# Absolute value of the spread positions two steps later and pinned in ScalarE's order, and nine buffers for the projection's loads

## The chip, the core and the metric

The kernel runs on one core of a Trainium2 chip, in fp32. The metric is the device time of one launch in microseconds; the median of three runs is given. TensorE is written PE below (PEld: its weight loads), VectorE DVE, ScalarE ACT, GpSimd POOL and SyncE SP.

## The reference, cut to what matters

Two layers on 32 images of 96 x 56 x 56. The first is an inverted bottleneck with residual; the second an attention by spectrum and a deformable convolution:

```python
# layer 0
h = silu(bn(conv1x1(x, fake_quant(w1))))           # 96 -> 576
h = silu(bn(depthwise3x3(h, fake_quant(w2))))
s = sigmoid(se_w2 @ silu(se_w1 @ h.mean((2, 3)) + se_b1) + se_b2)
x = x + bn(conv1x1(h * s, fake_quant(w3)))         # 576 -> 96
# layer 1
ca, sa = ...            # channel and spatial attention, from rfft2(x) and x
y = x * ca * sa
aux = concatenate([y, coord, freq_e])              # freq_e from rfft2(y)
offset = conv3x3(aux, off_w) + off_b               # 9 taps, (x, y) each
gate = sigmoid(conv1x1(relu(conv3x3(aux, dg1_w) + dg1_b), dg2_w) + dg2_b)
y_base = conv3x3(y, base_w) + base_b
px, py = xx + offset[:, :, 0], yy + offset[:, :, 1]
sampled = grid_sample_taps(y, px, py)              # bilinear: weights 1 - |distance|, cut at 0
y_def = einsum('bcthw,oct->bohw', sampled, def_w) + def_b
z = (1 - gate) * y_base + gate * y_def
out = relu(batch_norm(z over all images) + x)
```

## The kernel before

**Bands.** The second layer runs in bands of eight rows, seven to an image, 224 in all, in the loop at the end of `layers` (counted 0 to 6 in an image; a turn of the work beside it, described below, starts two bands before the end of an image, and the example that is read closely, from about 2160 us on, is one such turn). For band n, two halves are sampled: `sample_tiles` multiplies blocks of the image with a table of bilinear weights (L700, PE) and copies the results out of PSUM (L704, ACT); `pack` copies channels into the free partitions (three L711, ACT); `deform` multiplies with the deformable weights (seven L719, PE: the first needs the L704 copies alone, the others the packed ones). `combine` (L745 to L748, DVE) mixes in gate and base convolution. `block_channels` makes the blocks (POOL copy L682, transposes L686, ACT copy L688).

**The positions, two bands ahead.** `find(n + 2)`, which is the generator `offsets`, runs during band n and is advanced one step at a time: one `next` at the band's start, then seven for each half, each beside one `pump`. At the band's end a loop runs it out. Its steps: the joint convolution (L582, nine matmuls, and the base convolution L611), the offsets to `at` (L630, DVE), to DRAM as `od` (L634, POOL), and from there as `ht` to 112 partitions (L646, SP, 252 KB: each position is spread over the possible source columns and rows). Then ACT takes the absolute distance (L649, Abs) and cuts it (L650, Relu of 1 - |d|), and the result goes to DRAM as `hd` (L653, on ACT's queue). `weights_load` reads it back as `wc` and `wr`, two loads each to a half (L664 and L665, SP, 252 KB each), and `weights` multiplies them (L671, DVE) to the table that L700 uses.

**What runs beside it.** `pump` also advances two streams over other images, each by its share of the band's slots: `first(b + 2)` is `hidden` (expansion L166 on PE, L170 on ACT; depthwise taps L257 and L259 on DVE; Silu L219 on ACT, whose store L221 is on ACT's queue) and `second(b + 1)` is `attend`: the projection (`project_loads` L307 on SP into the pool `hq`, five loads of 196 KB to a set, matmuls L323, ACT L325, POOL add L443), then the spectra (loads L351 on SP, matmuls L376, squares L360 on ACT, reductions L362 on DVE, copies L383 on ACT, and so on) and the maps of attention. `load_rows` fetches the next image's rows (L561, SP), `attend_rows` (L569, DVE) multiplies them in place.

**Who sets the order.** SP runs in the order of the program (`manual_schedule`). For the other engines a scheduler chooses an order at compile time, by its own estimate of when operands are ready[...]. Buffers are rings: an `hq` load has to wait until the matmul that read the buffer eight loads back is done. The convolutions and the sampling share six PSUM banks (`bank`, pool `mm`); `acc` and `pd` have one each.

## Time and profile before

| | us |
|---|---|
| median of three runs (lowest, highest) | 9928.33 (9917.45, 9945.53) |
| profiled execution | 9938.35 |
| its span | 9936.6 |
| PE busy | 8753.8 |
| DVE busy | 7220.3 |
| ACT busy | 5346.3 |
| POOL busy | 2785.4 |

The mean granted clock of PE in the profiled execution is 0.933. The DMA engines moved 1485.53 MB, 150 GB/s. The span is nearly uniform: images pass through it at about one in 290 us, all with the same order of work. So one image is read closely, and the sums of the whole run are divided by 32. A row of the timeline gives the start, the length, the engine, the line, the operation with output and input tiles, how many instructions were put together, and in brackets the idle time of the engine before it with what ended it. A line of the waits gives the same over the whole run: the sum, the number of waits and the longest.

### The profile page before, as it was taken

How to read it: one execution, taken by the hardware profiler on the slowest of the kernel's cores; microseconds unless marked ns; L12 is line 12 of the kernel's file. 1: busy time of each engine (PE TensorE's matmuls, PEld its weight loads, DVE VectorE, ACT ScalarE, POOL GpSimd, SP SyncE). 2: the span in 40 equal slices, each digit the busy share in tenths (PEclk: the TensorE clock that was granted, in tenths of full speed). 3: DMA queues.
4: the chain of work that ended last, by engine and by line, in shares of the span. 5: the costliest groups of instructions: out<-in, count | busy, mean ns of one | idle time of the engine just before them, and what ended most of it. 6: DMA issues, size and time to landing. Idle time of an engine off the chain costs nothing. (4 is left out here: it accounts for less than half of the span.)

```text
span 9936.6 us, 122378 instructions
## 1 busy us (share of the span) xinstructions
PE 8753.8 (88%) x43766; PEld 5029.2 (51%) x43766; DVE 7220.3 (73%) x6948; ACT 5346.3 (54%) x10262; POOL 2785.4 (28%) x2639
## 2 busy tenths in 40 slices
PE   6899999998999999999899989999999999999970
PEld 3455555555555555555555555555555555555550
DVE  6688777777777777877777877777777777778323
ACT  2355555555555555555555555555555555555443
POOL 1132323332322333232233233233323223322210
PEclk9899999999999999999999999999999999999985
DMA  3345555554555555555555555555545555545549
GB/s 93 108 134 144 147 148 151 149 139 132 148 148 150 152 150 134 148 143 150 153 147 146 140 142 149 151 146 148 143 134 149 148 151 152 148 132 145 129 142 418
DMA packets 1085588, 1485.53 MB, mean 150 GB/s; under 512 B 606670, under 2 KB 856222, under 8 KB 1072686
## 3 DMA queue, kind: packets, MB, share of 16 engines
q1 hardware_dynamic: 875011, 985.23, 38.2%
q10 hardware_dynamic: 153675, 329.79, 8.9%
q0 software_dynamic: 56288, 162.60, 6.7%
q8 instruction: 352, 5.77, 0.3%
q14 instruction: 262, 2.15, 0.1%
HBM read 1064.28 MB, written 412.65 MB: 149 GB/s over the span
## 5 line engine op out<-in xcount | busy, mean ns | idle before, releaser
L259 DVE SCALAR_TENSOR_TENSOR acch<-hp,w,acch 128x1512 f32<-128x1512 f32 (+1 forms) x2250 | 4231.6, 1881 | 34.6
L682 POOL COPY ybl<-yp 96x448 f32<-96x448 f32 x896 | 1201.2, 1367 | 2065.8 <-PE mm L686 2065.3
L719 PE MATMUL pd<-v,c_def 128*96 128x224 f32 (+1 forms) x6272 | 1491.5, 391 | 315.0 <-ACT v L711 175.1
L582 PE MATMUL mm<-yp,c_jointW 104*128 104x448 f32 x4032 | 1609.2, 550 | 3.5 <-DMA yp<-fqd 3.5
L719 PEld LDWEIGHTS pd<-v,c_def 128*96 128x96 f32 (+1 forms) x6272 | 1100.7, 181 | 644.0 <-ACT v L711 192.8
L700 PE MATMUL mm<-wc,yt 64*96 64x144 f32 x12544 | 1124.4, 296 | 90.6 <-DVE yb L616 43.9
L323 PE MATMUL mm<-hq,w3s 128*96 128x392 f32 (+1 forms) x2560 | 1038.2, 546 | 168.7 <-DMA hq<-h2d 160.5
L582 PEld LDWEIGHTS mm<-yp,c_jointW 104*128 104x128 f32 x4032 | 762.3, 191 | 761.5 <-issue 694.7
L166 PE MATMUL mm<-xt,w 96*128 96x392 f32 (+3 forms) x2688 | 1077.4, 536 | 46.0 <-issue 33.0
L704 ACT COPY v<-mm 96x288 f32<-96x288 f32 (+1 forms) x2688 | 1005.8, 440 | 152.6 <-PE mm L700 120.2
L700 PEld LDWEIGHTS mm<-wc,yt 64*96 64x96 f32 x12544 | 861.9, 160 | 400.9 <-issue 233.5
L170 ACT ACTIVATE hp<-mm,sh,inv 128x392 f32<-128x392 f32 (+2 forms) x1216 | 816.0, 673 | 221.0 <-PE mm L166 143.2
L611 PE MATMUL mm<-yp,c_base0W 96*64 96x448 f32 x4032 | 916.7, 551 | 0.0
L671 DVE TENSOR_TENSOR wc<-wc,wr 128x1008 f32<-128x1008 f32 x448 | 551.9, 1232 | 458.0 <-DMA wr<-hd 349.3
L219 ACT ACTIVATE acch<-acch,sh,inv 128x1568 f32<-128x1568 f32 x288 | 486.9, 1690 | 642.2 <-DVE acch L259 641.1
L711 ACT COPY v<-v 32x448 f32<-32x448 f32 x1344 | 755.3, 562 | 28.7
L323 PEld LDWEIGHTS mm<-hq,w3s 128*96 128x96 f32 (+1 forms) x2560 | 410.1, 175 | 705.3 <-issue 576.6
L634 POOL DMA_DIRECT2D od<-at x224 | 185.9, 830 | 2046.4 <-DVE at L630 1655.6
L443 POOL TENSOR_TENSOR o<-o,xc 96x392 f32<-96x392 f32 x256 | 395.1, 1543 | 958.4 <-ACT o L325 955.9
L397 PE MATMUL mm<-s,c_GV 112*112 112x464 f32 x1536 | 659.5, 571 | 4.5 <-ACT s L383 4.5
L688 ACT COPY yt<-mm 128x384 f32<-128x384 f32 (+1 forms) x896 | 347.3, 439 | 500.1 <-PE mm L686 484.2
L569 DVE SCALAR_TENSOR_TENSOR yp<-yp,ca,sab 96x448 f32<-96x448 f32 x255 | 157.2, 626 | 576.7 <-DMA yp<-x1d 409.8
(191 smaller groups left out, 9184.6 us busy)
## 6 DMA issues: line engine op xcount, KB each, us to landing
h2d<-acch ACTq DMA_DIRECT2D x288, 784.0 KB
wc<-hd SPq DMA_DIRECT2D x896, 252.0 KB
wr<-hd SPq DMA_DIRECT2D x896, 252.0 KB
hq<-h2d SPq DMA_DIRECT2D x1024, 196.0 KB
x<-x1d SPq DMA_DIRECT2D x768, 98.0 KB
ht<-od SPq DMA_DIRECT2D x224, 252.0 KB
hd<-ht ACTq DMA_DIRECT2D x224, 252.0 KB
xt<-in_x SPq DMA_DIRECT2D x64, 609.0 KB
```

What stands on the lines that cost most here:

```text
L166: nc.tensor.matmul(pt[p0 : p0 + w1.shape[1], : rows * W], w1, xts[hf][:, r0 * W : (r0 + rows) * W], start=True, stop=True)
L170: nc.scalar.activation(h1[lo:hi, row0 : row0 + rows, 1 : 1 + W], pt[lo:hi, : rows * W].rearrange("p (h w) -> p h w", h=rows), AF.Silu, bia ...
L259: nc.vector.scalar_tensor_tensor(acc[:, lo:hi], win, wk, acc[:, lo:hi], ALU.mult, ALU.add)
L323: nc.tensor.matmul(pt[:C, :EW], w3s[ps, ch], hq[ps], start=(i == 0), stop=(i == NCH - 1))
L397: nc.tensor.matmul(pt[: 2 * W, :n].rearrange("p (q u) -> p q u", q=NPB), w["GV"][:, g], m, start=(k == 0), stop=(k == 1))
L582: nc.tensor.matmul(view, weights[:, k], yp[:channels, r0 : r0 + RB, dx + PD - 1 : dx + PD - 1 + W], start=(k == 0), stop=(k == NTAP - 1))
L611: nc.tensor.matmul(pb[k % 2 * BC : (k % 2 + 1) * BC, :BW].rearrange("p (h w) -> p h w", h=RB), w["base"][:, k], yp[:C, r0 : r0 + RB, dx + ...
L682: nc.gpsimd.tensor_copy(yb[:, :, s], blocks)
L700: nc.tensor.matmul(pt[k][:C, (t - lo) * KP : (t - lo + 1) * KP], yt[ps, t], s[ps, t * KP : (t + 1) * KP], start=True, stop=True)
L704: nc.scalar.copy(v[:C, :, lo:hi, k].rearrange("c k t p -> c t k p"), pt[k][:C, : (hi - lo) * KP].rearrange("c (t k p) -> c t k p", t=hi - ...
L711: nc.scalar.copy(v[C:, 1 + 2 * i : 3 + 2 * i], v[i * QC : (i + 1) * QC, KA:])
L719: nc.tensor.matmul(out.rearrange("c q (t x) -> c t q x", x=TS), p["w"]["def"][ks, k], v[ks, k].rearrange("c t s (r x) -> c t (s r) x", r=T ...
```

## The change

The Abs is called after six `yield`s in place of four, so it is two steps later among the 15 `next`s of a band: it was called in step 13 and is now called after the last, and the Relu with it. The store of `hd` falls from step 14 to the loop that runs the generator out at the band's end. The load of `ht` stays in step 9. `keep_in_program_order` binds the Abs behind the ScalarE instruction that was traced just before it, in order alone; `p` gets the entry `tc` for that. The pool `hq` has nine buffers in place of eight.

```diff
@@ def offsets @@
     nc.sync.dma_start(ht.rearrange("q n k -> q (n k)"), src)
-    for _ in range(4):
+    for _ in range(6):
         yield
-    nc.scalar.activation(ht, ht, AF.Abs, bias=w["blk"])
+    p["tc"].keep_in_program_order(nc.scalar.activation(ht, ht, AF.Abs, bias=w["blk"]))
     nc.scalar.activation(ht, ht, AF.Relu, bias=w["one"], scale=-1.0)
     yield
@@ def layers @@
-        p = {"dp": ctx.enter_context(tc.tile_pool(name="l1d", bufs=3, space=DRAM))}
+        p = {"tc": tc, "dp": ctx.enter_context(tc.tile_pool(name="l1d", bufs=3, space=DRAM))}
...
-        pools(tc, ctx, p, None, (("xt", 2), ("acch", 2), ("pl", 2), ("w3s", 1), ("hq", 8), ("o", 2), ("x2", 3),
+        pools(tc, ctx, p, None, (("xt", 2), ("acch", 2), ("pl", 2), ("w3s", 1), ("hq", 9), ("o", 2), ("x2", 3),
```

## The prediction

> **What bounds the kernel now.** I read the busy times first, then the waits, then one image's timeline on TensorE beside ScalarE and SyncE, then the windows view for the granted clock.

> ```profile
> PE 8753.8 (88%) x43766; PEld 5029.2 (51%) x43766; DVE 7220.3 (73%) x6948; ACT 5346.3 (54%) x10262; POOL 2785.4 (28%) x2639
> ```

> TensorE (PE) is busy 88% of the span, VectorE 73%, ScalarE 54%. A change of ScalarE's order can only pay through TensorE's idle time, and through the clock that an idle TensorE loses. Who lets it idle:

> ```profile
> ACT ht L649 <- DMA ht<-od: 736.3, 186, 9.8
> ...
> PEld pd L719 <- ACT v L711: 192.8, 74, 8.4
> ...
> PE mm L323 <- DMA hq<-h2d: 160.5, 66, 7.7
> ...
> PE pd L719 <- ACT v L704: 138.2, 35, 6.2
> ```

> The columns are total us, number of waits, longest. ScalarE stands 736.3 us at the Abs (L649), waiting for the spread positions to land. That is 23 us in each of 32 images, but ScalarE is not the bound; what counts is the smaller sum in TensorE's own rows: the deform matmuls (L719) that wait for ScalarE's copies (L711, L704), and the project matmuls (L323) that wait for their loads. In the image whose bands run from about 2160 to 2453 us, TensorE's gaps over 1.5 us are four, here called A to D:

> ```profile
> 2202.08 4.02 PE L323 MATMUL mm<-hq,w3s 128*96 128x392 f32 x10 [1.15 <-DMA hq<-h2d]
> ...
> 2241.32 5.25 PE L323 MATMUL mm<-hq,w3s 128*96 128x392 f32 x10 [4.78 <-DMA hq<-h2d]
> ...
> 2289.96 2.55 PE L719 MATMUL pd<-v,c_def 128*96 128x224 f32 x6 [8.18 <-ACT v L711]
> ...
> 2399.87 1.89 PE L376 MATMUL mm<-c_FU,x 112*112 112x116 f32 x8 [4.43 <-POOL x L356]
> ...
> 2450.13 3.30 PE L719 MATMUL pd<-v,c_def 96*96 96x224 f32 x8 [4.35 <-ACT v L704]
> ```

> The bracket is the idle time before the row and what ended it. A is the second row (with 1.15 us more before the first), B the third, C the fourth, D the fifth. ScalarE in the same stretch:

> ```profile
> 2240.78 0.78 ACT L649 ACTIVATE ht<-ht,c_blk 112x576 f32<-112x576 f32 x1 [6.15 <-DMA ht<-od]
> ...
> 2285.42 0.77 ACT L649 ACTIVATE ht<-ht,c_blk 112x576 f32<-112x576 f32 x1 [6.34 <-DMA ht<-od]
> ...
> 2289.34 1.74 ACT L711 COPY v<-v 32x448 f32<-32x448 f32 x3
> ...
> 2447.47 0.78 ACT L649 ACTIVATE ht<-ht,c_blk 112x576 f32<-112x576 f32 x1 [2.76 <-DMA ht<-od]
> ```

> At B and D the Abs itself holds the copies: at B the L711 copies that the deform matmuls need stand behind a 6.34 us wait, at D four L704 copies stand behind 2.76 us.

> ```profile
> 2281.00:2300.00 19.00, 10.82 (x33) 6.42 (x32) 16.79 (x15) 8.36 (x15) 0.00 (x0) 0.64 0.47 126
> 2445.00:2457.00 12.00, 7.65 (x40) 5.38 (x37) 10.17 (x8) 4.29 (x9) 2.43 (x2) 0.72 0.64 152
> ```

> In the last three columns (granted clock, DMA share, GB/s) the clock is 0.64 around B and 0.72 around D. Ten project matmuls take 5.25 us after A and 4.02 us after the short gap: a gap costs its length and slow work behind it.

> [...] copies whose data are ready stand behind the Abs. [...] Here the spread load (252 KB) is issued behind four weight loads of 252 KB and takes a median of 9.5 to 11.8 us to its last packet in five of the seven bands, 3.4 and 3.5 us in bands 3 and 4, where fewer loads stand ahead of it. [...]

> **The change part by part.** It adds no instruction: in the compiled order each engine has as many as before, and SP's order is the same.

> *Abs two steps later.* Compared band by band with the old order, the static order of ScalarE repeats in 28 of 32 images. By band of this image, named by the band whose positions are found (its Abs runs two bands earlier, so band 0's is the first of the example, at 2201 us):
> - Bands 0 and 5: the Abs keeps its place, so the 7.6 us wait in band 0 stays.
> - Band 1: two instructions (L325, L170) go ahead of it. Worth nothing on TensorE, as A waits for loads.
> - Band 2 (gap B): one L711 copy, an L170, an L360 and an L383 go ahead; two L711 copies still follow. The landing (2285.4) still ends the wait, but behind it stand fewer instructions. From 2285.42 to 2289.96 is 4.5 us now; without one L711 (0.56), one L360, and one L383 it is about 2 us less.
> - Bands 3 and 4: the Abs falls 25 and 16 us later, past its landing. There was 0 and 0.9 us of wait to win. The store of the result is later too (2322 to about 2340 in band 3), and SP's weight loads behind it with it; their multiply runs at 2362.8, so they have some 10 us of slack. Cost taken 0; without that slack each microsecond would show at L671, and behind it at the sampling matmuls L700.
> - Band 6 (gap D): four L704 copies (1.29 us) go ahead of the Abs. They could start at 2444.7, when L688 ends, instead of 2448.15. L719 then waits for the next thing, the L711 copies (1.74 us) and the yp rows whose load and multiply (L569) end near 2450.5 for the following conv.

> *Side effect.* The scheduler places other instructions anew. In band 2 the Silu L219 moves from 2274.34 to between L688 (2266.76) and four L704 copies (2267.66), though its last depthwise tap on VectorE is ready only about 2271.7. So a new in-order wait of about 4 us stands on ScalarE with four PSUM copies behind it, and TensorE runs out of PSUM banks: I estimate a new gap of 3.8 us at about 2268. Also in band 2 the first L360 goes ahead of the Abs, so that the next DFT loads are issued about 6 us earlier (2280 in place of 2286.66). VectorE's multiply L671 comes one tap earlier in bands 0 and 1; in band 5 L569 goes ahead of L616, which makes L616 1.4 us later, and L700 waits for it.

> *Ninth buffer.* Each project load waits for the matmul nine back in place of eight, one matmul (some 0.4 to 0.66 us) earlier. SP sits in such loads for 25.45 us from 2160.41; everything behind it (weights, spread positions) is issued 0.66 us earlier, and one load of 196 KB comes into a stretch in which the DMA is idle.

> Sum for one image:
> - A: 0.66 us earlier issue at the 4.78 gap, as much again from the 1.15 gap: -1.3 (0 to -2.0).
> - B: -2.0 behind the landing, -0.7 for the earlier issue, and +1.1 for what of the new L219 gap isn't absorbed. Most of it is: TensorE's work before B ends at 2281.8 and could end at 2285 without a loss, as the landing is what ends B. -1.6 (+2.5 to -6).
> - C: L376 about 1.2 us earlier by the earlier loads, L616 later: -0.3 (+1.5 to -3).
> - D: gap from 4.35 to about 3.0, and half of the 2 us that the slow clock costs behind it (14 L719 matmuls take 2.81 us at full clock, 4.49 to 5.54 after such gaps), at an even chance: -2.3 (-1.0 to -4.1).

> That is -5.5 us for an image. About 30 of the 32 have this pattern: -165 us. The profiled execution took 9938.35 us (span 9936.6), so 9773; it lay 10.0 us above the median of the runs (9928.33), so I predict 9765 for the median.

> **The rivals.**
> - *Shrunk gaps keep the clock* (0.14). If B and D fall below what costs the clock, each saves 2 to 3 us more: -9.5 an image, -285 us, 9645. For: half-clock time is 1338 us in 158 windows, so it is a large sum. Against: the gaps stay at 3 us and more.
> - *The stall only changes place* (0.14). The spread load lands behind four weight loads, whatever ScalarE does, and the first project matmul waits for the first load of a set, which the ninth buffer doesn't touch. Then only D's 0.5 to 1 us is left: 9905 to 9935. For: band 0 and 5 unchanged, SP's order the same.
> - *Slower: the Silu parked ahead of the PSUM copies in band 2* (0.17). Place: ScalarE between L688 and the four L704, at about 2267. Price: 3.8 us of TensorE idle and 2.5 us for the clock it costs, 6.3 us an image. It decides when more than about 4 us of it reach B's end, because A, C and D together bring 3.9. All of it: +2.4 an image, +72 us, 10000; most of it: 9975. For: [...] the banks are six. Against: the 8.18 us of idle right behind it.

> **How the numbers follow.** The forecast has 0.55 and its own range is 9690 to 9855 (-2.5 to -8 an image). The range over the cases goes from 9645 to 9960: it leaves out the worst of the slower case and little of the best. A change under 0.3% (30 us) can't be told from none. Faster: 0.55 + 0.14 + a part of the second rival (0.03) = 0.72; same: 0.11; slower: 0.17.

> **What would show it.** In the waits, L649 on its load should fall from 736 us to about 500, L719 on L711 and L704 by a third or more, L323 on its loads by 20 to 40 us, and L704 behind a waiting L219 should appear. In the timeline, D should shrink to about 3 us, B to 6 or 7, and a new gap of about 4 us should stand some 20 us ahead of B. I am wrong if B ends later after its start, if the clock around 2270 in this image falls, or if L323 still waits as long.

## The result, and the profile after

The changed kernel takes 9790.16 us in the median (9779.04 to 9798.13, four runs), the kernel before on the same chip 9936.93 (9917.45 to 9954.24; four runs, of which the table above has the first three): a ratio of 0.9852, 95% interval 0.9829 to 0.9875. The profiled execution of the changed kernel has a span of 9792.0 us at a mean granted clock of 0.937.

Its busy times, in the first part of the page:

```profile
PE 8810.8 (90%) x43766; PEld 5029.2 (51%) x43766; DVE 7212.9 (74%) x6948; ACT 5381.4 (55%) x10262; POOL 2646.4 (27%) x2639
```

The work is the same and TensorE is busy for a larger part of a shorter span. It is also busy 57.0 us longer than before with as many matmuls, so some of them run slower. The waits of the changed kernel (sum, number, longest):

```profile
DVE wc L671 <- DMA wr<-hd: 597.5, 176, 17.8
...
ACT ht L649 <- DMA ht<-od: 347.1, 107, 9.0
...
PEld pd L719 <- ACT v L711: 187.2, 105, 4.8
...
PE pd L719 <- ACT v L711: 152.9, 71, 4.6
...
PE mm L323 <- DMA hq<-h2d: 101.9, 56, 6.3
```

Half of ScalarE's wait at the Abs is gone (736.3 us before), and the project matmuls wait a third less (160.5). L719 on L704 fell from 138.2 to 14.7. But L719 on L711 fell little, and VectorE's multiply L671 waits 597.5 us for its loads. In the kernel before it waited 349.3:

```profile
DVE wc L671 <- DMA wr<-hd: 349.3, 151, 21.8
```

TensorE's timeline in one image of the changed kernel shows the four gaps in their new size, and three that were not there:

```profile
2505.02 5.25 PE L323 MATMUL mm<-hq,w3s 128*96 128x392 f32 x10 [3.50 <-DMA hq<-h2d]
...
2535.97 2.05 PE L700 MATMUL mm<-wc,yt 64*96 64x144 f32 x12 [1.36 <-ACT v L704]
...
2551.89 1.75 PE L719 MATMUL pd<-v,c_def 128*96 128x224 f32 x8 [1.11 <-ACT v L711]
...
2594.19 1.68 PE L166 MATMUL mm<-xt,w 96*128 96x392 f32 x2 [2.03 <-ACT yt L688]
...
2660.01 1.05 PE L376 MATMUL mm<-c_FU,x 112*112 112x116 f32 x8 [0.32 <-POOL x L356]
...
2666.82 1.16 PE L700 MATMUL mm<-wc,yt 64*96 64x144 f32 x8 [1.87 <-ACT hp L170]
...
2711.37 4.79 PE L719 MATMUL pd<-v,c_def 128*96 128x224 f32 x12 [2.70 <-ACT v L711]
```

A is the first row (4.78 before), B the third (8.18), C the fifth (4.43), D the last (4.35). The second, fourth and sixth rows are new. For B these two images overstate the change: over the 27 images of the table below, TensorE's wait for L711 in B's band averages 5.72 us before and 2.76 after.

For the sums I cut the whole run into bands at the gate's matmul L727 and averaged 27 images, band by band, from TensorE's records. In each field stand the band's length and, behind it, TensorE's idle time in it, in us. B falls into band 0, C into 3, D into 4, A into 6. The columns behind the first two belong to experiments below; the last one also has the swap of two VectorE instructions that is described there. Each column is one profiled execution. A second trace of the kernel before (the run hq9 below) has 292.06 us an image and bands up to 0.43 us from the first column, and the chips differ by up to 0.5%, so differences of half a microsecond in a band are not read.

| band | before | changed | nine buffers alone | pin and nine, old place | seven steps | seven, swap, ten buffers |
|---|---|---|---|---|---|---|
| 0 | 48.58, 6.32 | 45.58, 3.22 | 46.02, 3.96 | 46.61, 3.65 | 42.64, 1.64 | 45.11, 2.25 |
| 1 | 35.67, 1.65 | 38.59, 3.04 | 35.43, 1.60 | 37.84, 2.54 | 35.68, 1.90 | 34.84, 1.59 |
| 2 | 35.54, 1.28 | 36.15, 1.44 | 35.33, 1.19 | 34.93, 0.42 | 35.65, 0.87 | 35.35, 0.92 |
| 3 | 45.43, 4.22 | 43.52, 2.01 | 45.62, 4.26 | 42.58, 2.45 | 43.35, 2.38 | 42.85, 2.37 |
| 4 | 34.44, 4.56 | 32.71, 2.98 | 34.15, 4.38 | 32.22, 2.90 | 30.49, 2.19 | 30.74, 2.39 |
| 5 | 44.43, 1.75 | 42.82, 0.56 | 43.01, 0.54 | 42.44, 0.37 | 43.78, 0.50 | 43.15, 0.00 |
| 6 | 48.43, 4.73 | 47.92, 4.24 | 47.63, 4.20 | 47.63, 4.22 | 47.67, 4.02 | 43.19, 1.55 |
| image | 292.53, 24.51 | 287.30, 17.48 | 287.20, 20.14 | 284.25, 16.56 | 279.27, 13.50 | 275.22, 11.07 |

From before to changed an image loses 7.0 us of idle time but only 5.2 us of length. Bands 0, 3, 4, 5 and 6 win 8.8 us together, bands 1 and 2 give back 3.5. The time at half clock with TensorE at work stays at 22.4 and 23.5 us, but it moves: in band 1 it rises from 1.3 to 4.4 us. By an estimate from the 12 sampling matmuls shown below (2.05 us at half clock, 0.98 at full), these 3.2 us more cost about 1.6 us, so that band 1, 2.9 us longer, has 1.4 us more idle time and the rest in slower matmuls.

### The profile page after: what moved, and what is told of

Same layout as the page of the kernel before. It is cut to its first block, busy times and chain, and to the rows that moved or that the text cites. A ratio compares the mean times of both kernels' runs of the same rounds, so it can differ in the third digit from the quotient of the medians.

```text
span 9792.0 us, 122438 instructions
## 1 busy us (share of the span) xinstructions
PE 8810.8 (90%) x43766; PEld 5029.2 (51%) x43766; DVE 7212.9 (74%) x6948; ACT 5381.4 (55%) x10262; POOL 2646.4 (27%) x2639
## 5 line engine op out<-in xcount | busy, mean ns | idle before, releaser
L259 DVE SCALAR_TENSOR_TENSOR acch<-hp,w,acch 128x1512 f32<-128x1512 f32 (+1 forms) x2250 | 4264.4, 1895 | 33.4
L682 POOL COPY ybl<-yp 96x448 f32<-96x448 f32 x896 | 1107.4, 1263 | 2047.5 <-PE mm L686 2047.0
L582 PE MATMUL mm<-yp,c_jointW 104*128 104x448 f32 x4032 | 1643.7, 560 | 6.2 <-DMA yp<-fqd 3.5
L719 PE MATMUL pd<-v,c_def 128*96 128x224 f32 (+1 forms) x6272 | 1435.4, 379 | 175.6 <-ACT v L711 152.9
L719 PEld LDWEIGHTS pd<-v,c_def 128*96 128x96 f32 (+1 forms) x6272 | 1055.9, 174 | 472.6 <-ACT v L711 187.2
L700 PE MATMUL mm<-wc,yt 64*96 64x144 f32 x12544 | 1138.6, 298 | 148.7 <-ACT hp L170 54.4
L582 PEld LDWEIGHTS mm<-yp,c_jointW 104*128 104x128 f32 x4032 | 782.8, 196 | 799.0 <-issue 734.2
L166 PE MATMUL mm<-xt,w 96*128 96x392 f32 (+3 forms) x2688 | 1105.2, 549 | 73.8 <-ACT yt L688 39.8
L323 PE MATMUL mm<-hq,w3s 128*96 128x392 f32 (+1 forms) x2560 | 1029.1, 541 | 118.2 <-DMA hq<-h2d 101.9
L671 DVE TENSOR_TENSOR wc<-wc,wr 128x1008 f32<-128x1008 f32 x448 | 560.7, 1252 | 767.0 <-DMA wr<-hd 597.5
L700 PEld LDWEIGHTS mm<-wc,yt 64*96 64x96 f32 x12544 | 863.8, 160 | 487.7 <-issue 219.5
L704 ACT COPY v<-mm 96x288 f32<-96x288 f32 (+1 forms) x2688 | 999.5, 440 | 180.1 <-PE mm L700 136.4
L170 ACT ACTIVATE hp<-mm,sh,inv 128x392 f32<-128x392 f32 (+2 forms) x1216 | 815.9, 673 | 242.0 <-PE mm L166 171.3
L219 ACT ACTIVATE acch<-acch,sh,inv 128x1568 f32<-128x1568 f32 x288 | 487.6, 1693 | 660.5 <-DVE acch L259 646.6
L711 ACT COPY v<-v 32x448 f32<-32x448 f32 x1344 | 755.1, 562 | 29.7
L323 PEld LDWEIGHTS mm<-hq,w3s 128*96 128x96 f32 (+1 forms) x2560 | 403.3, 173 | 651.4 <-issue 492.9
L688 ACT COPY yt<-mm 128x384 f32<-128x384 f32 (+1 forms) x896 | 351.5, 441 | 531.0 <-PE mm L686 527.7
L166 PEld LDWEIGHTS mm<-xt,w 96*128 96x128 f32 (+1 forms) x2688 | 370.3, 184 | 485.4 <-issue 304.2
```

Of the source, the lines that this page charges most:

```text
L166: nc.tensor.matmul(pt[p0 : p0 + w1.shape[1], : rows * W], w1, xts[hf][:, r0 * W : (r0 + rows) * W], start=True, stop=True)
L170: nc.scalar.activation(h1[lo:hi, row0 : row0 + rows, 1 : 1 + W], pt[lo:hi, : rows * W].rearrange("p (h w) -> p h w", h=rows), AF.Silu, bia ...
L259: nc.vector.scalar_tensor_tensor(acc[:, lo:hi], win, wk, acc[:, lo:hi], ALU.mult, ALU.add)
L323: nc.tensor.matmul(pt[:C, :EW], w3s[ps, ch], hq[ps], start=(i == 0), stop=(i == NCH - 1))
L582: nc.tensor.matmul(view, weights[:, k], yp[:channels, r0 : r0 + RB, dx + PD - 1 : dx + PD - 1 + W], start=(k == 0), stop=(k == NTAP - 1))
L682: nc.gpsimd.tensor_copy(yb[:, :, s], blocks)
```

## The experiments

All kernels are compared by their ratio to the kernel before, run on the same chip beside them, since that kernel's own median lay between 9887 and 9937 us on the chips used.

### The parts of the change

The first run was meant to have nine buffers and nothing else.

> Nine buffers alone, Abs where it was; the order of instructions on every engine is that of before. Theory M (the moved Abs carries the gain, because PSUM copies no longer stand behind it): 20 to 50 us under before, TensorE idle for L323 on its loads down from 160 us to about 110, Abs wait L649 still above 650 us, gap C (L376 on POOL) still 100 us or more over the run. Rival H (the earlier project loads carry the gain): 100 us or more under before, Abs wait down towards 400 us.

The kernel run under this name still had eight buffers, that is, it was the kernel before. Its ratio, 1.000 (0.9989 to 1.0011), tells nothing of the buffer; it shows how well two equal kernels agree. The run with nine, later:

```diff
-        pools(tc, ctx, p, None, (("xt", 2), ("acch", 2), ("pl", 2), ("w3s", 1), ("hq", 8), ("o", 2), ("x2", 3),
+        pools(tc, ctx, p, None, (("xt", 2), ("acch", 2), ("pl", 2), ("w3s", 1), ("hq", 9), ("o", 2), ("x2", 3),
```

> Nine buffers and nothing else: the kernel before with that one number changed (the run called hq9 had kept eight). The scheduler moves a few ScalarE and VectorE instructions with it. Theory I (the ninth buffer is worth about 1% wherever the Abs stands, as it was with six and with seven steps): 60 to 120 us under before, project loads issued ahead of the band's first matmul, gap A down to about 3 us. Rival J (it is worth something only once the Abs is out of the way): within 30 us of before.

Measured: 0.9854 (0.9818 to 0.9889), 145 us, more than the 60 to 120 us of theory I; of the theories of the first run, H has the size. One more buffer brings as much as the whole change. By the table it shortens bands 0, 5 and 6 (B, and the stretch of the projection) and nothing else; C and D stay at 4.21 and 4.37 us. The Abs waits less, 586.9 us in place of 736.3, and TensorE less for L711 (175.1 us before):

```profile
ACT ht L649 <- DMA ht<-od: 586.9, 176, 7.5
...
PE pd L719 <- ACT v L711: 112.5, 37, 7.5
```

The Abs stands where it stood, except in one band, where it now stands ahead of two more instructions. So this comes from its load, which lands earlier, and not from its order.

The other half, the Abs two steps later and pinned, with eight buffers:

> Abs two steps later and pinned, eight buffers. Theory M: 90 to 130 us under before; gaps before L719 on L711/L704 halved, L323 on its loads still about 150 us. Rival H: at most 40 us under before, as the spread load still lands late and gap B stays near 8 us.

Measured: 0.9961 (0.9943 to 0.9979), 39 us. It is far from the 90 to 130 us of M. H has the size (at most 40) but not the place: B shrank (band 0 from 48.58 to 45.87 us) without the earlier loads, while band 1 grew from 35.67 to 39.37.

Then the place without the pin, and the pin without the new place, both with nine buffers:

> As the changed kernel without the pin; the scheduler then puts thousands of ScalarE instructions in other places. Theory M, if what counts is only that the Abs is called two steps later: within 0.5% of the changed kernel. Rival P (the pin carries it, since the scheduler drags the Abs forward again): half of the gain or more is lost, 9860 us or more.

> Nine buffers and the pin, with the Abs called where it was before. In the compiled order the pin alone puts the Abs behind the four L704 copies at D, behind L325 in the projection, and parks the Silu ahead of L704, all as in the changed kernel; an Abs wait stays ahead of fewer instructions. Theory P (the pin does the work, the two steps add little): within 0.4% of the changed kernel. Rival S (the two steps are needed, so that at B and in the projection fewer PSUM copies stand behind the Abs): less than half of the changed kernel's gain over nine buffers alone.

The first gives 0.9902 (0.9884 to 0.9920), between its two forecasts, and slower than nine buffers alone; the second 0.9824 (0.9787 to 0.9861), within 0.3% of the changed kernel, as theory P has it. Without the pin the waits at C and D are back:

```profile
PE pd L719 <- ACT v L704: 140.7, 34, 6.4
...
PE mm L376 <- POOL x L356: 127.9, 32, 4.4
```

With the pin, at the old place, they are gone but for 14.7 and 25.8 us (bands 3 and 4 in the table). So the pin, and not the two steps, takes away C and D. The two steps bring nothing that shows (0.9824 without them, 0.9852 with them), and rival S asked for a part of a gain over nine buffers alone that the changed kernel does not have.

C went with an order that the scheduler changed by the way. ScalarE's half L273 of the attention map's sigmoid stands ahead of the next L170 and Silu in all the pinned kernels, and VectorE's half L274 ahead of a depthwise tap (L259, 1.84 us) that it stood behind before. VectorE before, then in the changed kernel:

```profile
2374.17 1.84 DVE L259 SCALAR_TENSOR_TENSOR acch<-hp,w,acch 128x1568 f32<-128x1568 f32 x1
2375.93 0.18 DVE L274 TENSOR_SCALAR sa<-sa 112x56 f32<-112x56 f32 x1
```

```profile
2638.51 0.19 DVE L274 TENSOR_SCALAR sa<-sa 112x56 f32<-112x56 f32 x1 [0.36 <-ACT sa L273]
```

POOL, which multiplies with that map (L356), starts 1.1 us behind the end of L273 in place of 2.2, on average over the images. No run moved these two instructions alone, so this cause is read from the orders and not shown. Part of C came back in the same band: TensorE waits 1.8 us an image at the L700 of the sixth row above.

### What was given back

Band 1 is 2.9 us longer in the changed kernel. There, on VectorE and on ScalarE, in the image shown above:

```profile
2586.75 1.21 DVE L671 TENSOR_TENSOR wc<-wc,wr 128x1008 f32<-128x1008 f32 x1 [7.74 <-DMA wr<-hd]
```

```profile
2588.60 1.01 ACT L399 ACTIVATE sq<-mm 112x464 f32<-112x464 f32 x2 [6.60 <-DVE s L400]
```

The multiply waits 7.74 us for its loads with the spectral add L400 behind it, ScalarE's square L399 waits for the add, and the copies L688 stand behind the square: that ends the 2.03 us gap at L166 above. Before the change that L400 stood ahead of the multiply, which then waited 1.24 us:

```profile
2323.13 0.64 DVE L400 TENSOR_TENSOR s<-sq 112x464 f32<-112x464 f32 x1 [0.91 <-ACT sq L399]
2325.01 1.21 DVE L671 TENSOR_TENSOR wc<-wc,wr 128x1008 f32<-128x1008 f32 x1 [1.24 <-DMA wr<-hd]
```

The experiment swaps the two in each image and leaves the order of every other engine as it is (an order-only edge in every second call; `adds` lists the L400 instructions; shortened here):

```diff
-    nc.vector.tensor_tensor(wc, wc, wr, ALU.mult)
+    i = nc.vector.tensor_tensor(wc, wc, wr, ALU.mult)
...
+    p["tc"].add_manual_dep(i.ins, p["adds"][-2].ins.name, NoSync)
```

> The changed kernel with one pair of VectorE instructions swapped in each image: the multiply L671 that waits 7.7 us for its wr load goes behind the second spectral add L400, as it stood before the change; every other engine keeps the changed kernel's order. Theory L (what is given back in the stretch after B comes from this multiply holding L400, hence ScalarE's L399 and the PSUM banks): that stretch 1.5 to 3 us shorter in each image, 45 to 90 us under the changed kernel, TensorE gaps at L166 on L688 gone. Rival B (the landing of wr itself bounds the stretch, whatever waits for it): within 15 us of the changed kernel.

Measured: 0.9807 (0.9783 to 0.9830) against 0.9852, 0.45% or some 44 us. Theory L holds in size, at its low end. In place it holds in part: in the profiled execution band 1 is only 1.0 us shorter, and bands 0 and 6 are 0.6 and 0.7 us shorter too, little more than the traces differ by themselves. TensorE's wait at L166 in band 1 falls from 1.21 to 0.08 us, but its wait at L416 for VectorE's L413, which comes behind the swapped pair, rises from 1.41 to 2.32. In the same place of an image of this run:

```profile
2841.71 0.64 DVE L400 TENSOR_TENSOR s<-sq 112x464 f32<-112x464 f32 x1 [1.08 <-ACT sq L399]
...
2843.78 1.21 DVE L671 TENSOR_TENSOR wc<-wc,wr 128x1008 f32<-128x1008 f32 x1 [1.42 <-DMA wr<-hd]
```

A second cause may be the Silu that the prediction's slower rival rested on. ScalarE in the changed kernel:

```profile
2533.85 1.69 ACT L219 ACTIVATE acch<-acch,sh,inv 128x1568 f32<-128x1568 f32 x1 [2.61 <-DVE acch L259]
```

It stands there 2.61 us with the four L704 copies behind it, and TensorE loses 1.36 us (the second row of the timeline above) and then runs at half clock (granted clock 0.50 from 2536 to 2538 us): 12 sampling matmuls in 2.05 us, which take 0.98 us at a granted clock of 1.00 in most other places of the image. The experiment orders this one Silu behind those copies (`copies` lists the L704; shortened):

```diff
+        if u == 2:
+            tc.add_manual_dep(silu.ins, p["copies"][-5].ins.name, NoSync)
```

> The changed kernel with the Silu of one unit ordered behind the PSUM copies L704 that it stood ahead of (some other ScalarE places move with it: three L711 copies now stand behind the Abs in place of two). Theory S (the parked Silu costs the 1.4 us gap and about 3 us of half clock that the trace shows at L700, and little of it is absorbed): 60 to 130 us under the changed kernel. Rival A (as predicted, most of it is absorbed by the wait that ends B): within 30 us.

Measured: 0.9800 (0.9778 to 0.9823), 0.52% or some 51 us better than the changed kernel: between the two forecasts. The table's measure has band 0 only 0.3 us shorter, and band 1 2.2 us shorter. So B did absorb it, as predicted, and it came back one band later. The 0.52% is not this Silu's alone: the scheduler also moved another Silu back to its place before the change, and a stretch of VectorE's instructions ahead of the adds L400, and TensorE's wait at L166 in band 1 fell from 1.21 to 0.28 us, the same wait that the swap removes.

### Further along the same way

With seven steps the Abs is called in the loop that ends the band:

```diff
-    for _ in range(6):
+    for _ in range(7):
```

> Abs three steps later (in the loop that runs the generator out) and pinned, nine buffers. Theory M: the waits on the spread load fall further (L649 under 250 us), TensorE gaps B and D shrink a little more, but the wr loads behind it are later, so that L671 waits longer; 0 to 30 us under the changed kernel. Rival W (L671 on VectorE behind the later hd is now the bound of the stretch after B): slower than the changed kernel by 20 to 60 us.

Measured: 0.9629 (0.9607 to 0.9651), more than twice the gain of the change, and far beyond what either theory gave. TensorE at B, and ScalarE:

```profile
2763.64 2.51 PE L719 MATMUL pd<-v,c_def 128*96 128x224 f32 x12 [0.39 <-ACT v L711]
```

```profile
2763.02 1.74 ACT L711 COPY v<-v 32x448 f32<-32x448 f32 x3
2764.78 0.78 ACT L649 ACTIVATE ht<-ht,c_blk 112x576 f32<-112x576 f32 x1
```

All three L711 copies now stand ahead of the Abs, where in the changed kernel two stood behind it. The parked Silu is gone from band 0 as well, since the compiled order has it behind the copies, and the half-clock time of an image falls from 23.5 to 14.3 us. At D, too, all three L711 copies now stand ahead of the Abs (band 4 is 2.2 us shorter). These changes came together, and no run separates them.

Two variants of it, with eight buffers and without the pin:

> Abs three steps later, pinned, with eight buffers; TensorE's order is that of the version with nine, ScalarE's and VectorE's differ in a few places. Theory I (the ninth buffer is worth about 2 us an image once no Abs stands ahead of L325): 50 to 90 us over the version with nine buffers (9600 to 9640). Rival N (the buffer itself is worth nothing, as with the Abs where it was, and the difference seen with six steps came from the scheduler): within 20 us of it (9530 to 9570).

> Abs three steps later, nine buffers, no pin. Theory P (the pin is what keeps the Abs behind the L704 copies at D; at B the call's place alone does it): 60 to 150 us over the pinned version (9610 to 9700), with L719 on L704 back at about 140 us and L376 on POOL at about 128 us. Rival Q (a late call is enough): within 25 us of 9549.

Measured: 0.9744 (0.9719 to 0.9769) and 0.9794 (0.9775 to 0.9814), both further over the pinned version with nine buffers than theories I and P gave. Without the pin the waits of P are back, 141.1 and 122.6 us. The ninth buffer is worth 1.15% here, 1.09% with six pinned steps and 1.46% alone. The pin is worth 1.65% here, 0.5% with six steps, and 0.3% at the old place, where the intervals overlap.

The swap of L671 on top:

> Seven steps, pinned, nine buffers, and the same swap of L671 and L400 as in the run that put it behind. Theory L: there the multiply waits 3.2 us in place of 7.7 us and TensorE loses only about 0.3 us at L166 on L688, so 0 to 25 us under the version without the swap (ratio to before 0.960 to 0.963). Rival (the swap saved its 0.45% by making L671 itself, or what is placed behind it, cheaper): again about 45 us.

Measured: 0.9624 (0.9590 to 0.9658), no difference that can be told, as theory L has it: with less wait there, nothing is left for the swap to give.

The last run tests why a buffer is worth so much. SP in the kernel before (start, length, and x10 rows for five loads):

```profile
2745.55 30.54 SPq L307 DMA_DIRECT2D hq<-h2d  x10
2776.15 0.62 SPq L664 DMA_DIRECT2D wc<-hd  x1
```

For most of the 30.54 us SP stands in the projection's loads until the first project matmul, at 2774.03, frees a buffer; the weight loads and the spread load wait behind it, while the DMA engines are nearly idle (a share of 0.01 from 2763.1 to 2771.1 us). The windows view of the same stretch (granted clock, DMA share, GB/s in the last three columns), before and with nine buffers, each cut at the same distance from the band's gate matmul:

```profile
2759.10:2763.10 4.00, 4.00 (x19) 1.47 (x16) 0.07 (x1) 1.29 (x3) 0.00 (x0) 1.00 0.32 103
2763.10:2767.10 4.00, 3.98 (x38) 3.06 (x36) 0.55 (x1) 3.82 (x10) 1.06 (x2) 1.00 0.00 0
2767.10:2771.10 4.00, 4.00 (x26) 2.88 (x27) 1.12 (x4) 3.43 (x8) 0.00 (x0) 1.00 0.02 4
```

```profile
2715.10:2719.10 4.00, 4.00 (x20) 1.50 (x17) 0.12 (x1) 1.25 (x2) 0.00 (x0) 1.00 0.45 170
2719.10:2723.10 4.00, 3.99 (x40) 3.05 (x38) 0.50 (x1) 3.87 (x10) 1.06 (x2) 1.00 0.00 0
2723.10:2727.10 4.00, 4.00 (x26) 2.89 (x26) 1.18 (x4) 3.37 (x8) 0.00 (x0) 1.00 0.02 4
```

In the first window nine buffers move 67 GB/s more for 4 us, 268 KB, which is the one further load of 196 KB and some. Behind it the engines are idle for 8 us in both. A tenth buffer should use that (cut out of the line of the pools):

```diff
-("hq", 9), ("o", 2)
+("hq", 10), ("o", 1)
```

> Seven steps, pinned, the swap of L671 and L400, ten buffers for the projection's loads, paid for in memory by one buffer in place of two for the projection's output. TensorE's order is that of the version with nine. Theory F (each further buffer lets one more load of 196 KB land in the idle DMA time ahead of the projection, so that the DMA-bound stage ends sooner): 0.5 to 1% under the version with nine, ratio to before 0.953 to 0.958, gap A at 2 us or less. Rival G (nine already fill what is idle there, or the one output buffer makes L325 wait for its store): 0.960 or more.

Measured: 0.9486 (0.9465 to 0.9507), a median of 9431.52 us, the fastest of all and 1.4% under the version with nine. Theory F holds, with a size that was too small. SP no longer waits for a matmul at this place:

```profile
2624.02 12.52 SPq L307 DMA_DIRECT2D hq<-h2d  x10
2639.52 0.62 SPq L664 DMA_DIRECT2D wc<-hd  x1
```

The weight loads are issued 8.7 us ahead of the first project matmul (2648.18), where before they came 2.1 us behind it. In the waits of this run A is gone, and so is nearly all of the Abs's wait (306.1 us with nine buffers and the swap). But ScalarE has a new one, at the projection's copy L325, which waits for the single output buffer to be stored:

```profile
ACT o L325 <- DMA x1d<-o: 407.9, 101, 8.6
...
ACT ht L649 <- DMA ht<-od: 42.4, 43, 3.7
...
PE mm L323 <- DMA hq<-h2d: 3.1, 6, 1.5
```

So rival G's wait came, but TensorE's matmuls wait only 2.7 us for L325 in the whole run. Part of the Abs's wait may only have moved there. Ten buffers with two output buffers were not run.

## Why the prediction was right, and where its steps were not

The forecast was 165 us of gain, 9765 us; measured were 147 us and 9790.16. That the sum came out is luck, because its errors cancel. It gave some 2.0 of the 5.5 us of an image to the ninth buffer (A, and 0.7 us at B) and the rest to ScalarE's order. Run apart, the buffer alone brings 145 us, and the Abs with its pin 39 us with eight buffers and nothing that can be told on top of nine (0.9852 against 0.9854).

- **What bounds the kernel** holds: the versions follow TensorE's idle time and the clock behind it, not ScalarE's wait. Six pinned steps with eight buffers halve the Abs's wait, from 736.3 to 371.4 us, and win 0.39%.
- **The ninth buffer (A)** is the term that was mis-sized: -1.3 us an image at A and -0.7 at B, counted as 0.66 us of earlier issue. That issue is right: with nine buffers the first weight load follows the first project matmul by 1.46 us in place of 2.12. What was not counted is that a whole load moves out of the projection's stage, where the DMA engines are busy for a share of 0.85 (2779.1 to 2827.1 us, before), into idle time ahead of it, and that the spread load behind it lands earlier for all the bands of the stage. Alone it gives -5.3 us an image by the table (-4.5 by the ratio): -1.4 in band 5, -0.8 in band 6 and -2.6 at B.
- **B** was given to the Abs's new place, -1.6; band 0 measures -3.0. Earlier landing alone gives -2.6, the Abs and the pin alone -2.7, both together -3.0. Here the two remedies for one wait do not add. The wait itself was to fall to 6 or 7 us in the image that was read; that image, with 8.18 us, lies well above the average of 5.72, and on average 2.76 are left.
- **C** at -0.3 was too small in band 3 (-1.9), and **D** at -2.3 about right in band 4 (-1.7). The prediction put C down to earlier loads and D to the Abs's later place. Both need the pin, as the runs without it show, and earlier loads alone leave C as it was (4.20 us before, 4.21 with nine buffers alone, as TensorE's wait for POOL in band 3).
- **The multiply L671** was the step that is missing. The prediction listed it one tap earlier in two bands, at no cost, and did not list its move ahead of L400. Its loads land when they landed before (it starts 51.2 us behind the start of band 0 before and 50.8 after, on average), while everything ahead of it is earlier, so it waits 5.6 us in place of 0.5 with L400 behind it. By the table's measure the swap takes back 1.3 of the 3.5 us of bands 1 and 2, and the run with the moved Silu 2.6; the two overlap.
- **The parked Silu**, the slower rival, was real and in its place. With what moved along with it, it costs some 1.7 us an image (0.52%), not 6.3. TensorE's gap is 1.36 us, not 3.8.
- **That the stall only changes place** explains bands 1 and 2 and no more. **Shrunk gaps that keep the clock** did not come with this change (22.4 and 23.5 us at half clock), but with seven steps (14.3 us).
- **ScalarE's table loads** are 131 in the traces of both kernels, of 1.28 us each: the later Abs and Relu add none.

Left open: why band 0 is longer with ten buffers (45.11 us against 42.82 with nine and the swap; it has 2.6 us more at half clock and 0.6 us more idle time), how the swap's gain is spread over the bands, which of its changes gives seven steps their gain, and what the single output buffer costs. That six steps without the pin are slower than the old place without it (0.9902 against 0.9854) was not tested; there, too, the multiply stands ahead of L400 and waits 5.1 us an image in place of 0.7, and band 1 is 2.1 us longer.

## What to carry to other kernels

Look at the issuing queue ahead of a stage that waits for its loads: if it stands at a buffer while the DMA engines are idle, try one more buffer. Here it moved 268 KB more in 4 us of that time, a whole load and some, and the spread load behind it in the queue landed earlier too (the Abs waited 586.9 us in place of 736.3); alone it brought 1.46%. Look also for ready work that stands behind a late operand: in the changed kernel the sampling matmuls of four L704 copies had ended at 2532.84 us, and the copies started at 2535.54, behind the Silu that waited 2.61 us for VectorE; the run that ordered this Silu behind them, with what moved along, won 0.52%. And where a compiler chooses the order, an edit moves other instructions too, so compare the orders and run the parts apart before giving a gain to the part that was meant to bring it.

## What the runs showed of the hardware

| gap, us | gaps | half clock follows |
|---|---|---|
| 1.0 to 1.5 | 59 | 10 |
| 1.5 to 2.0 | 59 | 32 |
| 2.0 to 2.5 | 28 | 23 |
| 2.5 and more | 70 | 65 |

Shrinking gaps won little clock in this change (a mean granted clock of 0.933 before and 0.937 after): the gaps of 4 us and more fell from 97 to 9, but those of 1.5 to 2.5 us rose from 20 to 87, with half clock behind 11 and 55 of them, and the stretches at half clock went from 158 to 161.
